# Layer 0's softmax sums from added key blocks, and one values evacuation moved ahead of a gate

## The chip, the cores and the metric

The kernel runs on one core of a Trainium2 chip. The metric is the device time of one execution in microseconds (us). A core has several engines that each run their own instruction stream in order and wait for each other through semaphores: TensorE (PE, matrix products, with its weight loads shown as PEld), VectorE (DVE), ScalarE (ACT), GpSimd (POOL) and SyncE (SP, which issues the DMAs here). SBUF is the working memory, PSUM the memory that matrix products are written to.

## What is computed

The input x has 128 rows of 256 positions and 256 channels. Two layers each add an attention of a group-normalized x to x. Layer 0, which the change touches, is attention along the 256 positions of each row, with 8 heads of 32 channels, a bias computed from a second tensor z, and a sigmoid gate:

```python
m_norm = layer_norm(m, ln_m_w, ln_m_b)          # m = group norm of x
q = (m_norm @ Wq.T).reshape(B, s, i, h, c)      # k and v likewise
b = (z_norm @ Wb.T).transpose(0, 3, 1, 2)[:, None]
gate = jax.nn.sigmoid(m @ Wg.T + bg)
scores = jnp.einsum('bsihc,bsjhc->bshij', q, k) * scale + b
p = jax.nn.softmax(scores, axis=-1)
o = jnp.einsum('bshij,bsjhc->bsihc', p, v).reshape(B, s, i, h * c)
o = o * gate
return o @ Wo.T + bo
```

Layer 1 is a banded attention (each position sees 16 neighbours on either side) and is not changed. Everything is float32.

## The kernel before

**Phases.** A first phase (to about 300 us) computes the bias, keeps its exponential in the tile `eb`, and takes the statistics of x. Layer 0 follows, to about 2436 us, then layer 1. At the end a few sums are checked (a second, general kernel would run if a check failed; it does not run here).

**Layer 0's pairs.** Rows are handled two at a time, in 64 pairs; a `Pair` object (line 1148) holds a pair's tiles. Positions are cut into two blocks of 128 keys (index b). A pair has four blocks of work (r, c): row r of the pair, and head group c with four heads. For each:

- `scores` (line 1242): eight matmuls with 32-row weights, four of them side by side in the array, give the scores transposed, with keys on partitions and queries along the free dimension, into two PSUM tiles of two heads each. ScalarE's Exp (line 1258) turns each into a tile e of 128x1024 (two heads, two key blocks, 256 queries).
- `add_bias` (line 1262): e is multiplied by `eb`, because the exponential of a sum is a product. The first two heads' tile goes to VectorE, the second to GpSimd (line 1266).
- `apply` (line 1268): matmuls with 32 columns of weights give, for each head, the values product (e with v) and the ones-product (e with a block of ones), which is the softmax's sum repeated over the head's 32 partitions. Both accumulate over the two key blocks, so there are eight matmuls of each kind. Each shows as two records in the profile.
- `invert` (line 1282): VectorE's reciprocal of the sums.
- `gate` (line 1287): VectorE computes gr = (gate + 1) times the reciprocal (line 1292) and multiplies it with the values product (line 1295).

Around these, `out_row` and `keep_row` project a finished row and add the residual (line 1317, from the PSUM tile ps_y), and a later pair is prepared: `centre`, `scale` and `residual` on GpSimd, `moments` and `norm` on VectorE, a small power on GpSimd (`root`), transposes (`turn`), projections (`project`) and values (`values`, `keep_values`, line 1236, from the PSUM tile ps_v).

**The order of the work** is written out by hand (the loop from line 1388): the call order is each engine's instruction order, and one pair's loop body has four stages, each starting with the `scores` of one block. `apply`, `invert` and `gate` of a block stand one stage after its `scores`; GpSimd's `scale` stands before its multiplication in the second stage, `centre` before that in the first, `residual` after it in the third. `some(n)` adds n waiting statistics instructions on VectorE; every four pairs queue 17 of them.

**Buffers.** The PSUM tiles for transposes, projections, values and output rows share two buffers (`mm`), so the n-th such tile waits until the n-2nd has been read. The e tiles have two buffers for each of the two tags; the tiles of `turn` have two.

Of the kernel before, what the change touches and what calls it, by code (L numbers as in the profile page):

```python
# [9 lines left out]
F32 = mybir.dt.float32  # L10
AF = mybir.ActivationFunctionType
ALU = mybir.AluOpType
# [4 lines left out]
P = 128  # L17
# [756 lines left out]
def fast_kernel(  # L774
# [25 lines left out]
    nc = tc.nc  # L800
    S, I, C = x.shape
    CZ = z.shape[2]
    H = wbT.shape[1]
    D0 = C // H
# [3 lines left out]
    NB = I // P  # L808
    KC = C // P
    NP = S // 2  # L810
    N2 = 2 * I
# [9 lines left out]
    ones = const.tile([P, P], F32, name="ones")  # L821
# [155 lines left out]
    with tc.tile_pool(name="pre", bufs=2) as pre, tc.tile_pool(  # L977
        name="pre1", bufs=1
# [5 lines left out]
        for w, dst in ((wq, qb), (wk, kb)):  # L984
            for m in range(KC):
                ps = pps.tile([P, 512], F32, name="b_ps", tag="mm")
                for k in range(KC):
                    nc.tensor.matmul(
                        ps[:, 0:1], w[:, k, m * P : (m + 1) * P], lnb_c[:, k : k + 1],
                        start=(k == 0), stop=(k == KC - 1),  # L990
# [142 lines left out]
    HQ = P // D0  # L1133
# [5 lines left out]
    with tc.tile_pool(name="l0", bufs=2) as sb, tc.tile_pool(  # L1139
        name="l0s", bufs=4  # L1140
    ) as sm, tc.tile_pool(name="ps_mm", bufs=2, space=PSUM) as ps_mm, tc.tile_pool(
        name="ps_s", bufs=2, space=PSUM
    ) as ps_s, tc.tile_pool(name="ps_o", bufs=2, space=PSUM) as ps_o:

        def mm(name):
            return ps_mm.tile([P, 512], F32, name=name, tag="mm")

        class Pair:
# [39 lines left out]


            def turn(self, src, name):  # L1190
                dst = sb.tile([P, KC, N2], F32, name=name, tag=name)
                for k in range(KC):
                    ps = mm("ps_x")
                    for t in range(NT):
                        nc.tensor.transpose(ps[:, t * P : (t + 1) * P], src[:, t, k * P : (k + 1) * P], ident)
                    nc.scalar.copy(dst[:, k, :], ps)  # L1196
                return dst
# [62 lines left out]
                return self.es  # L1260

            def add_bias(self, r, c, es):
                for a in range(2):
                    h = c * HQ + 2 * a
                    eng = nc.vector if a == 0 else nc.gpsimd
                    eng.tensor_tensor(es[a], es[a], eb[:, h : h + 2], ALU.mult)  # L1266

            def apply(self, r, c, es):

                o = ps_o.tile([P, 2, I], F32, name="ps_ov", tag="o")  # L1270
                for what in range(2):
                    for b in range(NB):
                        for q in range(HQ):
                            h = c * HQ + q
                            w = self.v[:, r, b, h * D0 : (h + 1) * D0] if what == 0 else ones[:, :D0]
                            nc.tensor.matmul(  # L1276
                                o[q * D0 : (q + 1) * D0, what, :], w, es[q // 2][:, q % 2, b, :],
                                start=(b == 0), stop=(b == NB - 1),
                            )
                self.o = o  # L1280

            def invert(self, r, c):
# [69 lines left out]
        def some(n):  # L1352
            for _ in range(min(n, len(later))):
                later.pop(0)()
# [10 lines left out]
        def pair(p):  # L1365
            return Pair(p) if p < NP else Nobody()

        now, nxt, nn = pair(0), pair(1), pair(2)
# [17 lines left out]
        with tc.manual_schedule():  # L1386
            was, es = Nobody(), None
            for p in range(NP):
                nn3 = pair(p + 3)

                e = now.scores(0, 0)
                nn.centre()
                now.add_bias(0, 0, e)
                was.apply(1, 1, es)
                was.invert(1, 1)
                was.gate(1, 1)
                nxt.turn_g()
                nxt.project("gT", 0)
                nxt.project("gT", 1)
                some(2)  # L1400
                es = e

                e = now.scores(0, 1)
                nn.scale()
                now.add_bias(0, 1, e)
                now.apply(0, 0, es)
                now.invert(0, 0)
                was.out_row(1)
                was.keep_row(1)
                now.gate(0, 0)  # L1410
                nxt.turn_n()
                nxt.project("qT", 0)
                some(1)
                es = e

                e = now.scores(1, 0)
                now.add_bias(1, 0, e)
                nn.residual()
                now.apply(0, 1, es)
                now.invert(0, 1)  # L1420
                now.gate(0, 1)
                nxt.values(0)
                nxt.keep_values(0)
                nn.moments()
                nn.root()
                nxt.project("kT", 0)
                nxt.values(1)
                nxt.keep_values(1)
                es = e

                e = now.scores(1, 1)
                now.add_bias(1, 1, e)
                now.apply(1, 0, es)
                now.invert(1, 0)
                now.out_row(0)
                now.keep_row(0)
                now.gate(1, 0)
                nn.norm(0)
                nn.norm(1)
                nxt.project("kT", 1)  # L1440
                nxt.project("qT", 1)
                some(2)
                es = e
                was, now, nxt, nn = now, nxt, nn, nn3
            was.apply(1, 1, es)
            was.invert(1, 1)
            was.gate(1, 1)
            was.out_row(1)
            was.keep_row(1)
            some(len(later))  # L1450
# [17 lines left out]
    with tc.tile_pool(name="l1", bufs=2) as sb, tc.tile_pool(  # L1468
        name="l1s", bufs=4
    ) as sm, tc.tile_pool(name="ps1_mm", bufs=2, space=PSUM) as ps_mm, tc.tile_pool(  # L1470
        name="ps1_s", bufs=2, space=PSUM
# [63 lines left out]
        def scores1(d, r):  # L1535

            es = []
            for c in range(KC):
                ps = ps_s.tile([P, 2, 512], F32, name="ps_sc1", tag="s")
                for b in range(NB):  # L1540
                    for q in range(2):
                        rs = slice(q * D1, (q + 1) * D1)
                        nc.tensor.matmul(  # L1543
                            ps[:, q, b * W : (b + 1) * W],
                            d["kT"][rs, c, r * I + b * P : r * I + (b + 1) * P],
                            d["qT"][rs, c, r * I + q0(b) : r * I + q0(b) + W],
                            start=True, stop=True,
                        )
                e = sm.tile([P, 2, NB * W], F32, name="e1", tag=f"e{c}", bufs=3)
                nc.scalar.activation(e, ps[:, :, : NB * W], AF.Exp)  # L1550
                nc.gpsimd.tensor_tensor(e, e, bcast(bw.rearrange("p b w -> p (b w)"), 1, 2), ALU.mult)  # L1551
                es.append(e)
            return es
# [56 lines left out]
        for p in range(NP):  # L1610
# [3 lines left out]
            for r in range(2):  # L1614
                es = scores1(d, r)
# [34 lines left out]
@with_exitstack  # L1650
def mixer_kernel(ctx, tc, *args):

    nc = tc.nc
    keep = ctx.enter_context(tc.tile_pool(name="verdict", bufs=1))
    verdict = keep.tile([1, 1], mybir.dt.int32, name="verdict")
    fast_kernel(tc, *args, verdict)
    again = nc.values_load(verdict[0:1, 0:1], min_val=0, max_val=1)
    with tc.If(again > 0):
        general_kernel(tc, *args)
# [53 lines left out]
```

## Time and profile before

| what | value |
|---|---|
| median of 3 runs | 3873.88 us (3872.06 to 3875.07) |
| the profiled execution's own time | 3873.13 us |
| its span, first to last instruction | 3871.4 us |
| TensorE busy | 3610.3 us, 93% of the span |
| VectorE busy | 2232.6 us, 58% |
| GpSimd busy | 1794.0 us, 46% |
| ScalarE busy | 1390.9 us, 36% |
| granted TensorE clock, mean | 0.976 |
| one pair of layer 0 (1004.52 to 1037.88 us) | TensorE 32.29 us busy of 33.36; VectorE 24.20; GpSimd 18.45; ScalarE 14.13 |

The profile is of one execution. A row of its timeline has the start, the busy time, the engine, the source line, the operation, out<-in by the program's tile names, shapes and count; in brackets stand the idle time before it and what ended that. In the groups of the page the columns are busy time in total, mean in nanoseconds, and idle time before with its releaser. An instruction that stands still for something other than a semaphore shows as busy: its duration grows, and no wait is shown.

### The profile page before, as it was taken

Reading aid. Unit: us, or ns where it says so; the run is one execution under the profiler, and the core shown is the slowest. Engines: PE = TensorE matmul, PEld = TensorE weight load, DVE = VectorE, ACT = ScalarE, POOL = GpSimd, SP = SyncE. Lnnn points to the kernel's source line nnn. Section 1 sums busy time; section 2 is a strip of 40 time slices with the busy share of each in tenths; the row PEclk is TensorE's granted clock in tenths of the full one; section 3 lists DMA queues with packets and bytes.
Section 4 is the critical chain, followed back from the end, with each engine's and each line's share of the span. In section 5 each row is a group of like instructions: output and inputs, shape, how many; then the busy total and the mean of one; then the engine's idle time right before and its main releaser. Section 6 shows DMA issues by size and latency. Waiting matters only on the chain. (4 is left out here: it accounts for less than half of the span.)

```text
span 3871.4 us, 67673 instructions
## 1 busy us (share of the span) xinstructions
PE 3610.3 (93%) x29510; PEld 2214.9 (57%) x29510; DVE 2232.6 (58%) x3461; ACT 1390.9 (36%) x1937; POOL 1794.0 (46%) x869
## 2 busy tenths in 40 slices
PE   5659999999999999999999999799999999999996
PEld 3325555555555555555555555466666666666664
DVE  5755777777777777777777777333333333333335
ACT  2324444444444444444444444222222222222221
POOL 2364555555555555555555554333333333333332
PEclk8779999999999999999999999899999999999998
DMA  9940101110110011011101100211111111111111
GB/s 288 320 142 10 36 18 40 39 40 18 40 40 31 25 35 39 18 39 40 40 18 39 40 22 14 66 45 56 45 56 45 56 45 56 45 56 45 56 40 47
DMA packets 189924, 211.82 MB, mean 55 GB/s; under 512 B 6320, under 2 KB 172208, under 8 KB 189488
## 3 DMA queue, kind: packets, MB, share of 16 engines
q1 hardware_dynamic: 189616, 207.38, 17.1%
q8 instruction: 233, 3.82, 0.4%
q14 instruction: 75, 0.61, 0.1%
HBM read 138.68 MB, written 68.68 MB: 54 GB/s over the span
## 5 line engine op out<-in xcount | busy, mean ns | idle before, releaser
L1266 POOL TENSOR_TENSOR e<-e,eb 128x1024 f32<-128x1024 f32 x256 | 633.8, 2476 | 925.4 <-ACT e L1258 925.4
L1266 DVE TENSOR_TENSOR e<-e,eb 128x1024 f32<-128x1024 f32 x256 | 317.1, 1239 | 563.8 <-ACT e L1258 563.8
L1258 ACT ACTIVATE e<-ps_sc 128x1024 f32<-128x1024 f32 x512 | 496.8, 1022 | 259.0 <-PE ps_sc L1249 255.5
L1551 POOL TENSOR_TENSOR e<-e,bw 128x576 f32<-128x576 f32 x256 | 355.3, 1410 | 468.1 <-ACT e L1550 468.1
L1508 PE MATMUL ps_p<-xgT,w_in 128*128 128x512 f32 x1024 | 502.1, 614 | 0.1
L1571 DVE RECIPROCAL rv<-ps_su 128x256 f32<-128x256 f32 x128 | 225.0, 1757 | 398.5 <-PE ps_su L1566 398.5
L1285 DVE RECIPROCAL rv<-ps_ov 128x256 f32<-128x256 f32 x256 | 448.0, 1750 | 0.0
L1493 POOL TENSOR_TENSOR xb<-xt,bout_r 128x1024 f32<-128x1024 f32 x64 | 151.4, 2367 | 406.1 <-DVE yo L1584 401.6
L1526 DVE TENSOR_TENSOR v<-ps_v,bv_r 128x512 f32<-128x512 f32 x128 | 88.5, 692 | 395.1 <-PE ps_v L1522 386.5
L1550 ACT ACTIVATE e<-ps_sc 128x576 f32<-128x576 f32 x256 | 152.8, 649 | 450.7 <-PE ps_sc L1543 449.9
L1249 PE MATMUL ps_sc<-qT,kT 32*128 32x256 f32 x4096 | 293.7, 400 | 0.0
L1249 PEld LDWEIGHTS ps_sc<-qT,kT 32*128 32x128 f32 x4096 | 185.3, 184 | 171.3 <-issue 165.7
L1230 PE MATMUL ps_v<-wv,xnT 128*128 128x256 f32 x1024 | 254.9, 392 | 26.1 <-DVE v L1236 26.1
L1276 PE MATMUL ps_ov<-e,v 128*32 128x256 f32 x4096 | 274.7, 385 | 3.2 <-DVE e L1266 2.4
L1508 PEld LDWEIGHTS ps_p<-xgT,w_in 128*128 128x128 f32 x1024 | 179.7, 190 | 166.9 <-issue 124.2
L1276 PE MATMUL ps_ov<-e,ones 128*32 128x256 f32 x4096 | 268.3, 379 | 0.0
L1310 PE MATMUL ps_y<-wo,oT 128*128 128x256 f32 x1024 | 257.1, 394 | 3.9 <-DVE oT L1295 3.9
L1215 PE MATMUL ps_p<-xgT,wg 128*128 128x512 f32 x512 | 238.2, 608 | 20.1 <-ACT xgT L1196 19.7
L1230 PEld LDWEIGHTS ps_v<-wv,xnT 128*128 128x128 f32 x1024 | 184.1, 189 | 124.6 <-DVE v L1236 78.3
L1219 ACT ACTIVATE kT<-ps_p,kb 128x512 f32<-128x512 f32 x128 | 88.0, 688 | 451.8 <-PE ps_p L1215 451.8
L1522 PE MATMUL ps_v<-w_in,xgT 128*128 128x256 f32 x1024 | 248.3, 385 | 0.0
L1215 PE MATMUL ps_p<-xnT,wq 128*128 128x512 f32 x512 | 245.7, 603 | 0.2 <-ACT xnT L1196 0.2
(145 smaller groups left out, 5558.5 us busy)
## 6 DMA issues: line engine op xcount, KB each, us to landing
xa<-in_x_dram SPq DMA_DIRECT2D x8, 4096.0 KB
xt<-in_x_dram SPq DMA_DIRECT2D x64, 512.0 KB
x<-xo SPq DMA_DIRECT2D x16, 2048.0 KB
xt<-x SPq DMA_DIRECT2D x64, 512.0 KB
out_dram<-yo SPq DMA_DIRECT2D x64, 512.0 KB
rsum<-rv SPq DMA_DIRECT2D x64, 16.0 KB
rsum<-rv SPq DMA_DIRECT2D x64, 8.0 KB
rs_all<-rsum SPq DMA_DIRECT2D x1, 1024.0 KB
```

The costliest lines, as they stand in the source:

```text
L1215: nc.tensor.matmul(ps, w[:, k, m * P : (m + 1) * P], getattr(self, src)[:, k, :], start=(k == 0), stop=(k == KC - 1),)
L1230: nc.tensor.matmul(self.ps_v[:, b * C : (b + 1) * C], self.xnT[:, k, t * P : (t + 1) * P], wv[:, k, :], start=(k == 0), stop=(k == KC - 1),)
L1249: nc.tensor.matmul(self.pss[q // 2][:, q % 2, b, :], self.kT[rs, c, r * I + b * P : r * I + (b + 1) * P], self.qT[rs, c, r * I : (r + 1) * I],
L1258: nc.scalar.activation(e, self.pss[a], AF.Exp)
L1266: eng.tensor_tensor(es[a], es[a], eb[:, h : h + 2], ALU.mult)
L1276: nc.tensor.matmul(o[q * D0 : (q + 1) * D0, what, :], w, es[q // 2][:, q % 2, b, :], start=(b == 0), stop=(b == NB - 1),)
L1285: nc.vector.reciprocal(self.rv[:, r, c, :], self.o[:, 1, :])
L1310: nc.tensor.matmul(self.ps_y[:, b * C : (b + 1) * C], self.oT[:, k, b * P : (b + 1) * P], wo[:, k, :], start=(k == 0), stop=(k == KC - 1),)
L1508: nc.tensor.matmul(ps, w_in[:, k, n * C + m * P : n * C + (m + 1) * P], xgT[:, k, :], start=(k == 0), stop=(k == KC - 1),)
L1522: nc.tensor.matmul(ps[:, b * C : (b + 1) * C], xgT[:, k, t * P : (t + 1) * P], w_in[:, k, 2 * C : 3 * C], start=(k == 0), stop=(k == KC - 1),)
L1551: nc.gpsimd.tensor_tensor(e, e, bcast(bw.rearrange("p b w -> p (b w)"), 1, 2), ALU.mult)
L1571: nc.vector.reciprocal(rv[:, r, :], su)
```

## The change

Three things change in layer 0. After each multiplication with `eb`, the same engine adds the two key blocks of the tile to a new tile `eboth` of 128x512 (one for each tag, two buffers). The ones-products run on that tile: four for each block of work instead of eight, with no accumulation. In the third stage the first values product is computed and evacuated before the gate of (0, 1) instead of after it; on TensorE this moves nothing, on VectorE the evacuation (line 1236) stands directly behind the reciprocal. The tiles of `turn` get one buffer instead of two.

```diff
-                dst = sb.tile([P, KC, N2], F32, name=name, tag=name)
+                dst = sb.tile([P, KC, N2], F32, name=name, tag=name, bufs=1)
...
                 for a in range(2):
                     h = c * HQ + 2 * a
                     eng = nc.vector if a == 0 else nc.gpsimd
                     eng.tensor_tensor(es[a], es[a], eb[:, h : h + 2], ALU.mult)
+                    both = sm.tile([P, 2, I], F32, name="eboth", tag=f"both{a}", bufs=2)
+                    eng.tensor_tensor(both, es[a][:, :, 0, :], es[a][:, :, 1, :], ALU.add)
+                    es.append(both)
...
-                for what in range(2):
-                    for b in range(NB):
-                        for q in range(HQ):
-                            h = c * HQ + q
-                            w = self.v[:, r, b, h * D0 : (h + 1) * D0] if what == 0 else ones[:, :D0]
-                            nc.tensor.matmul(
-                                o[q * D0 : (q + 1) * D0, what, :], w, es[q // 2][:, q % 2, b, :],
-                                start=(b == 0), stop=(b == NB - 1),
-                            )
+                for b in range(NB):
+                    for q in range(HQ):
+                        h = c * HQ + q
+                        nc.tensor.matmul(
+                            o[q * D0 : (q + 1) * D0, 0, :], self.v[:, r, b, h * D0 : (h + 1) * D0],
+                            es[q // 2][:, q % 2, b, :], start=(b == 0), stop=(b == NB - 1),
+                        )
+                for q in range(HQ):
+                    nc.tensor.matmul(
+                        o[q * D0 : (q + 1) * D0, 1, :], ones[:, :D0], es[2 + q // 2][:, q % 2, :],
+                        start=True, stop=True,
+                    )
...
                 now.invert(0, 1)
-                now.gate(0, 1)
                 nxt.values(0)
                 nxt.keep_values(0)
+                now.gate(0, 1)
                 nn.moments()
```

In the changed kernel the multiplication is line 1267, the addition line 1269, the values and ones-products lines 1278 and 1283, the reciprocal line 1292, the gate lines 1299 and 1302.

## The prediction

> **What bounds the kernel now.** I read the page's engine shares first (TensorE 93% busy), then the costliest groups, then the timeline of layer 0. All times are in us.
>
> ```profile
> L1266 POOL TENSOR_TENSOR e<-e,eb 128x1024 f32<-128x1024 f32 x256 | 633.8, 2476 | 925.4 <-ACT e L1258 925.4
> L1266 DVE TENSOR_TENSOR e<-e,eb 128x1024 f32<-128x1024 f32 x256 | 317.1, 1239 | 563.8 <-ACT e L1258 563.8
> L1285 DVE RECIPROCAL rv<-ps_ov 128x256 f32<-128x256 f32 x256 | 448.0, 1750 | 0.0
> L1276 PE MATMUL ps_ov<-e,ones 128*32 128x256 f32 x4096 | 268.3, 379 | 0.0
> ```
>
> The ones-products, which the change halves, hold TensorE for 268.3 in all. VectorE and GpSimd have long waits before their multiplications, so they look free. The timeline of one second stage (one of the four between two scores groups) shows whether they are:
>
> ```profile
> 1012.48 1.15 PE L1249 MATMUL ps_sc<-qT,kT 32*128 32x256 f32 x16
> ...
> 1014.71 1.23 DVE L1266 TENSOR_TENSOR e<-e,eb 128x1024 f32<-128x1024 f32 x1 [3.11 <-ACT e L1258]
> ...
> 1015.67 2.48 POOL L1266 TENSOR_TENSOR e<-e,eb 128x1024 f32<-128x1024 f32 x1 [2.98 <-ACT e L1258]
> 1015.86 1.75 DVE L1285 RECIPROCAL rv<-ps_ov 128x256 f32<-128x256 f32 x1
> ...
> 1017.52 0.63 DVE L1317 TENSOR_TENSOR xo<-ps_y,xt 128x512 f32<-128x512 f32 x1
> ...
> 1018.21 0.66 PE L1195 MATMUL ps_x<-ident,xn 128*128 128x128 f32 x4 [0.36 <-DVE xo L1317]
> ...
> 1020.59 0.50 PE L1249 MATMUL ps_sc<-qT,kT 32*128 32x256 f32 x4
> ```
>
> TensorE is full, but a VectorE chain runs close under it: exp, multiplication, reciprocal, evacuation of ps_y, and only then do the second transposes get their PSUM buffer (0.36 of wait already). I call the stages A (0,0), B (0,1), C (1,0), D (1,1). They take 7.96, 8.11, 8.99 and 8.30: 33.36 a pair, the same in every full pair. Offsets below count from a stage's first scores matmul. VectorE's multiplication starts at 2.24 and ends at 3.47, GpSimd's is asked for at 3.20 and ends at 5.68, and the reciprocal starts at 3.38.
>
> The view that decides is the end of layer 0, by engine:
>
> ```profile
> 2412.64 2.57 DVE L1266 TENSOR_TENSOR e<-e,eb 128x1024 f32<-128x1024 f32 x1
> ...
> 2418.47 3.29 DVE L1266 TENSOR_TENSOR e<-e,eb 128x1024 f32<-128x1024 f32 x1
> ```
> ```profile
> 2411.77 2.36 POOL L1266 TENSOR_TENSOR e<-e,eb 128x1024 f32<-128x1024 f32 x1 [0.47 <-ACT e L1258]
> 2418.33 2.34 POOL L1266 TENSOR_TENSOR e<-e,eb 128x1024 f32<-128x1024 f32 x1 [4.20 <-ACT e L1258]
> ```
>
> In these two blocks GpSimd's multiplication began ahead of VectorE's; no other VectorE multiplication of the 256 is longer than 1.3. VectorE's took 2.57 and 3.29 instead of 1.23, and ended 1.08 after GpSimd's end both times: it stood still until 0.14 before that end. In the other direction GpSimd's 2.48 against 2.35 undisturbed puts its start 0.14 before VectorE's end. The gate's first instruction (L1292) takes 0.79 instead of 0.41 where it meets that multiplication.
>
> [...]
>
> ```profile
> 2427.43:2430.84 3.41, 1.47 (x18) 0.50 (x10) 3.27 (x10) 0.00 (x0) 0.00 (x0) 1.00 0.01 2
> 2430.84:2434.25 3.41, 1.85 (x4) 1.50 (x5) 1.44 (x3) 0.00 (x0) 0.00 (x0) 0.50 0.02 5
> ```
>
> The columns are length, busy TensorE, weight loads, VectorE, ScalarE, GpSimd, granted clock. After a window with 1.47 busy the clock is 0.50.
>
> **The change part by part.**
>
> *Ones-products halved.* Values and ones products take 0.88 and 0.98 before the next matmul starts, 16 records each; 8 records fewer are 0.44. Over 256 blocks that is 113, all of it gained if nothing else binds.
>
> *VectorE's new addition,* 128x512, two SBUF inputs. Duration: oT's 256 elements take 0.424, the multiplication's 1024 take 1.225, so 512 take 0.69. It waits for its own multiplication (3.47), so it cannot ask before about 3.51. GpSimd asked for its multiplication at 3.20[...]. The addition is then blocked until 5.54 and ends at 6.23. Queued behind it in order is the reciprocal: 6.14 instead of 3.38, **2.76 later in every stage**. Bounds: 0.73 later if ports don't block it (0.69 plus 0.04), 2.76 if they do; I take 2.76, since the same engine, operation and operand kinds show it.
>
> *GpSimd's new addition.* Its 1024 elements take 2.37 (xb), 576 take 1.41, so 512 take 1.27. It runs at 6.09 to 7.36; the products that need it start in the next stage at about 1.96, so that wait is covered by two or more. But it pushes scale and residual to 7.32 to 9.67, and the gate's first instruction, asking at 7.92, is blocked until 9.53.
>
> *Stage A.* TensorE doesn't wait for VectorE here, and ScalarE is free for the xgT copies at 3.12, before the transposes end: 7.96 - 0.44 = 7.5. VectorE runs late: gate 9.53 to 10.40, two statistics to 11.07, which is 3.57 into B.
>
> *Stage B.* GpSimd asks at 3.20, now ahead: it runs 3.20 to 5.55, VectorE's multiplication 5.41 to 6.64, GpSimd's addition 6.50 to 7.77, VectorE's 7.63 to 8.32, reciprocal 8.23 to 9.98, ps_y out at 10.52. Before, the stage ended 2.44 after that evacuation: 12.96. Seventeen statistics entries fill twenty places in four pairs, so about one A in four has none; then VectorE is first (2.90 to 4.13), GpSimd 3.99 to 6.34, addition to 6.89, ps_y out 9.09, end 11.53. Mean 12.6.
>
> *Stage C.* Reciprocal to 7.89; the first values product, now ahead of the gate, is out at 8.48 (7.01 before); the second values product starts at 8.54 and the stage ends 1.92 later: 10.46. The move itself is worth up to 0.6 a pair in the old timeline (0.79 and 0.42 of gate no longer precede it); in the new one the gate would hold it until about 11. It moves no DMA: only the gate of (1,1) issues one, and SP's and GpSimd's queues keep their order. The gate's late result is needed 2.5 into D.
>
> *Stage D.* VectorE reaches D at 2.4, because statistics and the second values evacuation end late[...]. Multiplication 2.75 to 3.97, GpSimd's 3.83 to 6.18, addition 6.04 to 6.73, reciprocal to 8.39, ps_y out at 8.93, the q projection after it, end 1.81 after 8.99: 10.8.
>
> Sum 7.5 + 12.6 + 10.46 + 10.8 = 41.36 against 33.36: 8.0 a pair.
>
> *Clock.* In B TensorE has nothing from about 5.0 to 10.5[...]: 2.6 a pair.[...]
>
> *Buffers.* xgT and xnT keep one buffer each. xnT's last reader, D's q projection, stands before the next pair's copies in TensorE's own order by a whole stage, and xgT's by three; cost nothing, and the transposes' copies would wait if that cover were gone.
>
> Some 62 full pairs: (8.0 + 2.6) x 62 = 657 on the profiled execution's 3873.13, which is 0.75 under the median of the runs, so no correction: **4530**. Layer 1 stays.
>
> **Rivals.**
> 1. *Ports as above, but the clock stays up or its loss is hidden*: 3873 + 496 = 4369. For it: C and D wait for VectorE, so slower matmuls there may cost nothing. Against: scores and the last q projection of B lie on the chain.
> 2. *The addition follows its multiplication onto the ports at once, so only the 0.73 counts*: A 7.5; B 8.11 + 0.73 = 8.84; C: reciprocal to 5.86, values out at 6.45, second product from 6.51, end 1.92 later, 8.43; D: ps_y out at 6.41, the q projection at 6.47 where it stood at 6.49 anyway, 8.30. Sum 33.1, so 0.27 a pair less: 3856, **faster** by 0.4%. B and C grow one for one with the reciprocal's delay, D too from about 0.75, so it decides near 0.8 of delay. Against it: GpSimd is already asking when VectorE's multiplication ends (1015.67 against 1015.94)[...].
> 3. *No blocking of the addition, but the gate behind GpSimd's longer queue is late and reaches into B*: the gate of A would end some 0.5 to 1 after VectorE's turn in B. Rival 2's sum plus that is 3890 to 3920.
> 4. *GpSimd's addition becomes what TensorE waits for*: it would have to end after 1.96 of the next stage, and by the sums above it ends at least two earlier. A delay of 3 in all four stages would be 12 a pair; I give it no chance of its own.
>
> **How the numbers follow.** Main case 0.6, rival 1 0.27, rival 2 0.05, rival 3 0.08. About 0.2% (8 us) is what a measurement of this kernel tells from no change. The range holds main case and rival 1. Low end: rival 1's 4369 less 22, if B's fast order (12.96 - 11.53 = 1.43 shorter) comes in another quarter of the 62 pairs. High end: 4530 plus the clock's upper bound (0.8 x 62 = 50), plus B always in its slow order (0.36 x 62 = 22), plus 40 if the waits of 2 to 3 in C and D halve the clock too (0.65 a pair). That is 4350 to 4640. Faster 0.05 is rival 2; slower 0.93 is the rest but 0.02 for sums that cancel.
>
> **What would show it.** VectorE's additions (L1269) with a mean near 2.5 instead of 0.69; the reciprocal starting near 6.1 after the scores in A and C; waits of TensorE for xo in B and D and for v in C, each in the hundreds of us; TensorE busy well under 90% in layer 0, granted clock near 0.9 there; stage B longest. I would be wrong if L1269 on VectorE took 0.7, or if GpSimd's multiplication were the one that is delayed.

## The result and the profile after

The changed kernel takes 4455.52 us in the median (4454.62 to 4456.39, 4 runs), against 3874.48 us (3872.06 to 3875.1, 4 runs) for the kernel before: a ratio of 1.1501, with a 95% interval of 1.1481 to 1.1521. It is 15% slower, 581 us. The forecast was 4530 with a range of 4350 to 4640.

The costliest groups on the page of the changed kernel, with the columns of the page before (busy in total, mean in ns | idle before and its releaser):

```profile
L1269 DVE TENSOR_TENSOR eboth<-e 128x512 f32<-128x512 f32 x256 | 645.8, 2523 | 8.8
L1215 PE MATMUL ps_p<-xnT,wq 128*128 128x512 f32 x512 | 339.6, 799 | 376.0 <-DVE xo L1324 375.7
L1267 DVE TENSOR_TENSOR e<-e,eb 128x1024 f32<-128x1024 f32 x256 | 396.9, 1550 | 354.7 <-ACT e L1258 354.3
L1269 POOL TENSOR_TENSOR eboth<-e 128x512 f32<-128x512 f32 x256 | 429.9, 1679 | 20.1
L1230 PE MATMUL ps_v<-wv,xnT 128*128 128x256 f32 x1024 | 263.8, 402 | 143.5 <-DVE v L1236 143.5
L1299 DVE SCALAR_TENSOR_TENSOR gr<-gT,rv 128x256 f32<-128x256 f32 x256 | 349.8, 1366 | 2.3
```

VectorE's new addition takes 2523 ns in the mean. Its shortest is 691 ns: that is the work, and the rest is standing still. Before it there are only 8.8 us of idle time, because a blocked instruction counts as busy. TensorE now waits 375.7 us for the evacuation of ps_y (line 1324) and 143.5 us for that of ps_v (line 1236), where the same two evacuations cost it 22.2 and 26.1 us before. The chain of work that ended last, from the same page, runs largely over VectorE, on layer 0's lines (1269, 1292, 1267 and 1299 among them). The chain on the page before hardly reaches back into layer 0, so it gives no share to set beside this:

```profile
PE 45%; DVE 41%; issue 5%; ACT 4%; DMA 2%; POOL 2%; SPq 1%; ACTq 0%; POOLq 0%; DVEq 0%
```

A pair takes 42.6 us instead of 33.36. One second stage (B) in the timeline of the changed kernel; it is preceded by the end of A:

```profile
1027.76 2.36 POOL L1162 TENSOR_TENSOR xg<-xg,R_l 128x1024 f32<-128x1024 f32 x1
1027.98 1.15 PE L1249 MATMUL ps_sc<-qT,kT 32*128 32x256 f32 x16
...
1028.37 2.03 DVE L1299 SCALAR_TENSOR_TENSOR gr<-gT,rv 128x256 f32<-128x256 f32 x1
...
1031.17 2.35 POOL L1267 TENSOR_TENSOR e<-e,eb 128x1024 f32<-128x1024 f32 x1 [1.06 <-ACT e L1258]
1031.44 3.16 DVE L1267 TENSOR_TENSOR e<-e,eb 128x1024 f32<-128x1024 f32 x1
...
1033.60 2.12 POOL L1269 TENSOR_TENSOR eboth<-e 128x512 f32<-128x512 f32 x1
1033.65 0.66 PE L1195 MATMUL ps_x<-ident,xn 128*128 128x128 f32 x4 [0.73 <-ACT xnT L1196]
...
1034.64 1.63 DVE L1269 TENSOR_TENSOR eboth<-e 128x512 f32<-128x512 f32 x1
1036.19 1.75 DVE L1292 RECIPROCAL rv<-ps_ov 128x256 f32<-128x256 f32 x1
1037.86 0.62 DVE L1324 TENSOR_TENSOR xo<-ps_y,xt 128x512 f32<-128x512 f32 x1
...
1038.54 3.43 PE L1215 MATMUL ps_p<-xnT,wq 128*128 128x512 f32 x4 [4.24 <-DVE xo L1324]
...
1041.90 1.15 PE L1249 MATMUL ps_sc<-qT,kT 32*128 32x256 f32 x16
```

The gate of A (1028.37) stands still until GpSimd's scaling is done, so VectorE comes to B's multiplication 0.27 after GpSimd. VectorE's then takes 3.16 instead of 1.23, the two additions follow, GpSimd's (1033.60) ahead of VectorE's (1034.64), and TensorE has nothing for 4.24 us. What it does next, four records of the q projection, takes 3.43 us, most of it at half clock (0.51 from 1038.10 to 1041.53); at full clock, from 1018.54 in D, four take 1.98. The columns of the windows view are length, busy TensorE, weight loads, VectorE, ScalarE, GpSimd, and then the granted clock, the DMA engines' share and GB/s:

```profile
1034.70:1038.10 3.40, 0.00 (x0) 0.00 (x0) 3.40 (x3) 0.22 (x1) 1.02 (x1) 1.00 0.00 0
1038.10:1041.53 3.43, 2.99 (x4) 1.18 (x4) 1.47 (x4) 0.00 (x0) 0.00 (x0) 0.51 0.43 128
1041.53:1044.94 3.41, 3.41 (x43) 1.89 (x43) 0.81 (x1) 2.55 (x3) 0.00 (x0) 1.00 0.09 30
```

### The profile page after: what moved, and what is told of

It is laid out like the page before. It is cut to its first block, busy times and chain, and to the rows that moved or that the text cites. A ratio compares the mean times of both kernels' runs of the same rounds, so it can differ in the third digit from the quotient of the medians.

```text
span 4452.8 us, 64344 instructions
## 1 busy us (share of the span) xinstructions
PE 3670.1 (82%) x27462; PEld 2194.9 (49%) x27462; DVE 3035.3 (68%) x3717; ACT 1390.6 (31%) x1937; POOL 2192.6 (49%) x1125
## 4 chain that ended last, share of the span: by engine, by line
PE 45%; DVE 41%; issue 5%; ACT 4%; DMA 2%; POOL 2%; SPq 1%; ACTq 0%; POOLq 0%; DVEq 0%
PE ps_p L1515 11%; DVE eboth L1269 11%; DVE rv L1292 9%; DVE e L1267 9%; PE ps_p L1215 8%; PE ps_v L1529 5%; PE ps_y L1587 5%; DVE gr L1299 4%; PE ps_sc L1249 4%; PE ps_o L1573 4%; PE ps_sc L1550 3%; ACT e L1258 3%; DMA zt<-in_z_dram 2%; DVE xo L1324 2%; PE ps_su L1573 1%
## 5 line engine op out<-in xcount | busy, mean ns | idle before, releaser
L1269 DVE TENSOR_TENSOR eboth<-e 128x512 f32<-128x512 f32 x256 | 645.8, 2523 | 8.8
L1215 PE MATMUL ps_p<-xnT,wq 128*128 128x512 f32 x512 | 339.6, 799 | 376.0 <-DVE xo L1324 375.7
L1267 DVE TENSOR_TENSOR e<-e,eb 128x1024 f32<-128x1024 f32 x256 | 396.9, 1550 | 354.7 <-ACT e L1258 354.3
L1269 POOL TENSOR_TENSOR eboth<-e 128x512 f32<-128x512 f32 x256 | 429.9, 1679 | 20.1
L1230 PE MATMUL ps_v<-wv,xnT 128*128 128x256 f32 x1024 | 263.8, 402 | 143.5 <-DVE v L1236 143.5
L1215 PEld LDWEIGHTS ps_p<-xnT,wq 128*128 128x128 f32 x512 | 107.9, 233 | 529.8 <-DVE xo L1324 442.6
L1299 DVE SCALAR_TENSOR_TENSOR gr<-gT,rv 128x256 f32<-128x256 f32 x256 | 349.8, 1366 | 2.3
L1249 PE MATMUL ps_sc<-qT,kT 32*128 32x256 f32 x4096 | 336.3, 447 | 0.0
L1249 PEld LDWEIGHTS ps_sc<-qT,kT 32*128 32x128 f32 x4096 | 209.4, 209 | 223.9 <-issue 210.4
L1219 ACT ACTIVATE qT<-ps_p,qb 128x512 f32<-128x512 f32 x128 | 88.0, 687 | 633.8 <-PE ps_p L1215 633.8
```

The lines of the kernel that those rows point to most:

```text
L1215: nc.tensor.matmul(ps, w[:, k, m * P : (m + 1) * P], getattr(self, src)[:, k, :], start=(k == 0), stop=(k == KC - 1),)
L1230: nc.tensor.matmul(self.ps_v[:, b * C : (b + 1) * C], self.xnT[:, k, t * P : (t + 1) * P], wv[:, k, :], start=(k == 0), stop=(k == KC - 1),)
L1249: nc.tensor.matmul(self.pss[q // 2][:, q % 2, b, :], self.kT[rs, c, r * I + b * P : r * I + (b + 1) * P], self.qT[rs, c, r * I : (r + 1) * I],
L1269: eng.tensor_tensor(both, es[a][:, :, 0, :], es[a][:, :, 1, :], ALU.add)
L1299: nc.vector.scalar_tensor_tensor(gr, self.gT[:, c, r * I : (r + 1) * I], 1.0, self.rv[:, r, c, :], ALU.add, ALU.mult)
```

## The experiments

The theory under test: **VectorE's addition, with both operands in SBUF, stands still while GpSimd multiplies, as VectorE's multiplication did in two blocks of the kernel before (2.57 and 3.29 us instead of 1.23), and delays the reciprocal behind it; the halved clock adds to that.** In the prediction and the expectations this is the port theory. "Port" is the author's name; the traces show the standing still, and not what in the chip causes it. Rivals: the addition's own work in front of the reciprocal is enough, whatever it reads; the longer GpSimd queue is to blame; the moved evacuation, the halved products or the single buffers cost something; the clock's loss lies off the chain. All times are medians of 4 or 5 runs. The mean stage lengths come from the start of each group of scores products in the traces, without the first and last pairs:

| kernel | time | ratio to before (95%) | A | B | C | D | pair |
|---|---|---|---|---|---|---|---|
| before | 3874.5 | 1 | 7.96 | 8.12 | 8.99 | 8.30 | 33.36 |
| changed | 4455.5 | 1.1481 to 1.1521 | 7.53 | 13.44 | 10.98 | 10.64 | 42.59 |
| move alone | 3831.3 | 0.9871 to 0.9904 | 7.96 | 8.11 | 8.31 | 8.30 | 32.68 |
| no additions | 3750.0 | 0.9664 to 0.9696 | 7.53 | 8.12 | 7.88 | 7.87 | 31.38 |
| PSUM operand | 3860.7 | 0.9948 to 0.9976 | 7.53 | 8.64 | 8.46 | 8.43 | 33.06 |
| TensorE kept busy | 4328.5 | 1.1153 to 1.1190 | 7.53 | 12.05 | 10.41 | 10.44 | 40.42 |
| GpSimd's addition only | 3828.2 | 0.9868 to 0.9901 | 7.94 | 8.12 | 8.29 | 8.28 | 32.64 |
| VectorE's addition only | 4334.3 | 1.1173 to 1.1211 | 7.96 | 11.67 | 10.62 | 10.40 | 40.64 |
| late addition, late centring | 3763.5 | 0.9701 to 0.9733 | 7.53 | 8.12 | 7.88 | 7.97 | 31.49 |
| late addition alone | 4106.4 | 1.0586 to 1.0621 | 7.53 | 13.80 | 7.88 | 7.97 | 37.17 |
| GpSimd made to wait | 4049.4 | 1.0436 to 1.0471 | 7.53 | 10.93 | 8.84 | 8.86 | 36.15 |

### The move alone

```diff
                 now.invert(0, 1)
-                now.gate(0, 1)
                 nxt.values(0)
                 nxt.keep_values(0)
+                now.gate(0, 1)
```

> The kernel before with one edit: the first values evacuation stands ahead of the gate of (0, 1). Port theory (the additions cause the loss, the move is a gain): stage C 8.4 instead of 8.99, other stages as before, 0.5 to 0.6 a pair, so 3836 to 3845. Rival (the move delays a gate that something waits for): C no shorter or D longer, 3874 or more.

It took 3831.34 us, 43 less than before, all of it in C (8.31), so the move is a gain and not part of the loss. It is a little more than the 30 to 38 expected.

### No additions

```diff
                     eng.tensor_tensor(es[a], es[a], eb[:, h : h + 2], ALU.mult)
-                    both = sm.tile([P, 2, I], F32, name="eboth", tag=f"both{a}", bufs=2)
-                    eng.tensor_tensor(both, es[a][:, :, 0, :], es[a][:, :, 1, :], ALU.add)
-                    es.append(both)
...
-                        o[q * D0 : (q + 1) * D0, 1, :], ones[:, :D0], es[2 + q // 2][:, q % 2, :],
+                        o[q * D0 : (q + 1) * D0, 1, :], ones[:, :D0], es[q // 2][:, q % 2, 0, :],
```

> The changed kernel without both additions: the ones-products run on the first key block alone, so the sums leave out the second block. Port theory: TensorE saves 0.44 in each stage and nothing stands in front of the reciprocal; about 31.3 a pair, 3745 (3730 to 3770). Rival (half the ones-products, the single buffers or the move are to blame for the loss): well above 3874, up to the changed kernel's 4455.

It took 3750.00 us, as the port theory had it. The halved ones-products, the move and the single buffers together save 125 us; with the additions the kernel takes 705 us more. A, C and D each lose 0.43 of ones-products (0.44 was expected), C the move's 0.68 besides; only B stays at 8.12, where a chain over VectorE was under TensorE's work in the kernel before (0.36 us of wait for xo).

### An addition with a PSUM operand

```diff
+                    other = self.pss[0] if a == 0 else es[a]
-                    eng.tensor_tensor(both, es[a][:, :, 0, :], es[a][:, :, 1, :], ALU.add)
+                    eng.tensor_tensor(both, es[a][:, :, 0, :], other[:, :, 1, :], ALU.add)
```

> The changed kernel, with VectorE's addition taking its second operand from the PSUM tile of the scores (the raw scores of the second block instead of their weights), so same size, same place in the queue, same wait, but one SBUF input. Port theory: L1269 on VectorE near 0.69 instead of 2.52, reciprocal about 4.1 after the scores, and 3830 to 3890 in all. Rival (the addition's work and its wait on the multiplication in front of the reciprocal, whatever it reads): unchanged, 4400 to 4460.

It took 3860.68 us, 595 less than the changed kernel, with the same number of instructions on every engine. From its groups by line:

```profile
L1270 DVE TENSOR_TENSOR eboth<-e,ps_sc 128x512 f32<-128x512 f32 x256 | 176.0, 688 | 27.4 <-DVE e L1267 0.9
```

The addition takes 688 ns instead of 2523, and the reciprocal starts 4.17 (D) to 4.72 (A) after the scores. So it is neither the size, the place in the queue nor the wait on the multiplication: what costs is that both operands are in SBUF while GpSimd works (2523 ns; 688 with one of them in PSUM).

### TensorE kept busy

```diff
-                    for t in range(NT):
-                        nc.tensor.transpose(ps[:, t * P : (t + 1) * P], src[:, t, k * P : (k + 1) * P], ident)
+                    for again in range(1 + (warm if k else 0)):     # warm=6 in turn_n
+                        for t in range(NT):
+                            nc.tensor.transpose(ps[:, t * P : (t + 1) * P], src[:, t, k * P : (k + 1) * P], ident)
...
                 ps = mm("ps_p")
-                for k in range(KC):
+                for again in range(2 if which == "kT" else 1):
+                    for k in range(KC):
```

> The changed kernel with filler for TensorE in its gaps: the second group of transposes in B is done seven times, the k projections in C and D twice, all into the buffer they own. Theory that the halved clock lies on the chain: clock near 1.0 in layer 0, B's slow order 12.4, pair 40.4 instead of 42.6, 4320 (4300 to 4345). Rival (clock lost off the chain): clock near 1.0 and 4430 to 4470. If the filler itself delays B's fast order, up to 15 more than either.

It took 4328.53 us: repeated products that nobody needs make the kernel 127 us faster. The span and mean clock of its profiled execution (0.944 in the changed kernel):

```profile
core 0: 4326.7 us, clock 0.978
```

The standing still was left as it was (VectorE's addition still 2520 ns), so of the 581 us the halved clock is 127, or 2.17 of the 9.23 a pair, and the rest, 454, is there at full clock.

### One addition at a time

```diff
+                    if a == 1:     # a == 0 in the other run
                         both = sm.tile([P, 2, I], F32, name="eboth", tag=f"both{a}", bufs=2)
                         eng.tensor_tensor(both, es[a][:, :, 0, :], es[a][:, :, 1, :], ALU.add)
                         es.append(both)
...
+                        if q // 2 == 1 and b:     # == 0 in the other run
+                            continue
+                        src = es[2][:, q % 2, :] if q // 2 == 1 else es[q // 2][:, q % 2, b, :]
```

> The changed kernel with GpSimd's addition only: heads 2 and 3 of a block have two ones-products on the added tile, heads 0 and 1 four on the two key blocks; all sums complete. Port theory: the harm is in VectorE's addition, asked for while GpSimd multiplies; GpSimd's own delays only gates. TensorE saves 0.22 a stage and the move its 0.6: about 32.3 a pair, 3800 to 3825. Rival (the longer GpSimd queue is what costs, through the late gates): 3900 or more.

> The changed kernel with VectorE's addition only: heads 0 and 1 on the added tile, heads 2 and 3 on both key blocks; all sums complete. Port theory: reciprocal at about 6.1 in every stage as in the changed kernel, but gates end 1.2 earlier, so VectorE is ahead of GpSimd in B: A 7.7, B 10.7, C 10.9, D 10.3, 39.6 a pair, 4230 to 4310. Rival (VectorE's addition alone is harmless): under 3900.

With GpSimd's addition only it took 3828.19 us, with VectorE's only 4334.26. The harm starts with VectorE's: its reciprocal then starts 6.14 after the scores in A, B and D. GpSimd's addition alone does none: the time is that of the move alone (3831.34, overlapping intervals). Beside VectorE's it is not free, since the changed kernel takes 121 us more than the run with VectorE's only: the gate's first instruction stands still longer (1.37 in the mean instead of 0.50), VectorE's multiplication in B then comes second to GpSimd's (2.56 instead of 1.23), and B takes 13.44 instead of 11.67. Both runs were expected to save 0.22 of TensorE's time in each stage, and did not; A stayed at 7.94 and 7.96. This is the line for the ones-products on key blocks in the run with GpSimd's addition, from its groups by line, and the one of the changed kernel, which has halved ones-products throughout:

```profile
L1288 PE MATMUL ps_ov<-e,ones 128*32 128x256 f32 x2048 | 265.2, 379 | 0.0
```

```profile
L1283 PE MATMUL ps_ov<-eboth,ones 128*32 128x256 f32 x2048 | 158.5, 379 | 1.0 <-POOL eboth L1269 1.0
```

A block's eight ones-products are two rounds of four, which stand side by side in the array: in the kernel before, four records of 379 ns each take 0.40 us together (from 1014.44). Both lines have 2048 records. In the run with GpSimd's addition, 1024 more, on the added tile, stand beside those of the first round, and 265.2 us is what both rounds take (268.3 in the kernel before, with all 4096 records): two products of the second round are left out, and the two that stay take as long as four. In the changed kernel the whole second round is left out, and 158.5 us remain. VectorE's run missed its upper bound by 24 us; the excess lies in A, for this reason (7.96 instead of 7.7), and in B (11.67 instead of 10.7), where the q projection often took long too (3.53 us for four records; in the changed kernel 3.43 at mostly half clock and 1.98 at full clock).

### GpSimd made to wait

```diff
+                    if a == 1:
+                        tick = sm.tile([P, 4], F32, name="tick", tag="tick")
+                        eng.tensor_tensor(tick, es[2][:, 0, :4], mhalf[:, :4], ALU.mult)
                     eng.tensor_tensor(es[a], es[a], eb[:, h : h + 2], ALU.mult)
```

> The changed kernel with a small GpSimd instruction ahead of its multiplication that reads VectorE's new tile[...]; all the work is kept, and one instruction is added to each stage. Port theory (who asks first holds): L1269 on VectorE near 0.69, the reciprocal about 4.1 after the scores, GpSimd's multiplication 1.2 or more later than before, and 3860 to 3960 in all; the rest of the loss is GpSimd's late queue. Rival (the two engines together have too much work, in whatever order): 4300 or more.

It took 4049.44 us: less than half of the loss is left, but more than expected. The timeline of this run, C first, then B:

```profile
1005.00 0.69 DVE L1272 TENSOR_TENSOR eboth<-e 128x512 f32<-128x512 f32 x1
1005.61 1.75 DVE L1295 RECIPROCAL rv<-ps_ov 128x256 f32<-128x256 f32 x1
1005.77 0.20 POOL L1269 TENSOR_TENSOR tick<-eboth,mhalf 128x4 f32<-128x4 f32 x1 [4.54 <-DVE eboth L1272]
...
1005.93 2.35 POOL L1270 TENSOR_TENSOR e<-e,eb 128x1024 f32<-128x1024 f32 x1
...
1028.48 2.35 POOL L1162 TENSOR_TENSOR xg<-xg,R_l 128x1024 f32<-128x1024 f32 x1
1028.50 3.41 DVE L1270 TENSOR_TENSOR e<-e,eb 128x1024 f32<-128x1024 f32 x1 [0.67 <-ACT e L1258]
```

The addition now takes 0.69: GpSimd is held back by a semaphore until it is done (4.54 of wait), so no GpSimd instruction runs beside it. The expectation missed B. There GpSimd's late scaling starts 0.02 ahead of VectorE's multiplication, which then takes 3.41 (3.08 in the mean of all B stages) instead of 1.23.

### The addition later

```diff
-                    both = sm.tile([P, 2, I], F32, name="eboth", tag=f"both{a}", bufs=2)
-                    eng.tensor_tensor(both, es[a][:, :, 0, :], es[a][:, :, 1, :], ALU.add)
-                    es.append(both)
+                es += [None, None]
+                self.add_keys(es, 1)     # GpSimd's addition, behind both multiplications
...
-                nn.centre()              # these two lines not in the second run
                 now.add_bias(0, 0, e)
+                nn.centre()
...
                 now.gate(0, 0)           # and so behind the gate of every stage
+                now.add_keys(e, 0)       # VectorE's addition
```

> The changed kernel with VectorE's addition behind the gate of its stage instead of in front of the reciprocal, and GpSimd's centring of a later pair behind its multiplication and addition in A instead of in front (it ran in D). Port theory: [...]the reciprocal is at 3.4 again, and nothing reaches into the next stage: 31.3 a pair, 3745 to 3775, close to the kernel without additions (3750). Rival (VectorE and GpSimd have no room for the additions at any place): 3850 or more.

> As the run with the late addition, but the centring stays where it was. Port theory: in D VectorE's addition and four normalizations now meet GpSimd's addition and centring, VectorE comes late into A and then B[...]: B some 12 to 14.5, 4050 to 4180. Rival (only the place in front of the reciprocal matters): as the other, 3745 to 3775.

With both edits it took 3763.52 us, ratio 0.9717 (0.9701 to 0.9733): **faster than both kernels**, 2.8% under the kernel before, with the same computation as the changed kernel. The timeline of one C:

```profile
1015.78 1.23 DVE L1267 TENSOR_TENSOR e<-e,eb 128x1024 f32<-128x1024 f32 x1 [1.25 <-ACT e L1258]
...
1016.74 2.47 POOL L1267 TENSOR_TENSOR e<-e,eb 128x1024 f32<-128x1024 f32 x1 [1.42 <-ACT e L1258]
1016.92 1.75 DVE L1297 RECIPROCAL rv<-ps_ov 128x256 f32<-128x256 f32 x1
...
1018.59 0.63 DVE L1236 TENSOR_TENSOR v<-ps_v,vb_r 128x512 f32<-128x512 f32 x1
1019.13 0.41 DVE L1304 SCALAR_TENSOR_TENSOR gr<-gT,rv 128x256 f32<-128x256 f32 x1
1019.29 1.39 POOL L1274 TENSOR_TENSOR eboth<-e 128x512 f32<-128x512 f32 x1
...
1019.92 1.30 DVE L1274 TENSOR_TENSOR eboth<-e 128x512 f32<-128x512 f32 x1
```

The reciprocal and the evacuation of ps_v, both with a PSUM operand, now run during GpSimd's multiplication and take no longer for it (1.75 and 0.63; the shortest of the changed kernel are 1.74 and 0.62). VectorE's addition still stands still behind GpSimd's (1.30 instead of 0.69), but nothing urgent is queued behind it. The additions cost 13.5 us over the kernel without them.

Without the moved centring it took 4106.42 us, in the expected range. In the expected manner only in part: VectorE does come late from D into A, since its normalizations meet GpSimd's centring (0.91 for one in the mean, 0.42 in the changed kernel), but TensorE's largest wait is another. The timeline of that run:

```profile
1034.13 1.07 PE L1283 MATMUL ps_ov<-e,v 128*32 128x256 f32 x16 [1.97 <-DVE e L1267]
1038.57 1.08 PE L1288 MATMUL ps_ov<-eboth,ones 128*32 128x256 f32 x8 [3.37 <-DVE eboth L1274]
```

VectorE's addition of A itself lands so late that B's ones-products wait for it, 60 times in the run and 222.5 us in all.

## Why the prediction was right, and where its sum was off

**The mechanism and its sign were right.** The steps by their own numbers, from the scores of the stage, beside what the changed kernel's timeline shows:

| step | predicted | measured |
|---|---|---|
| reciprocal in A | 6.14 | 6.14 |
| gate of A done with its first instruction | 9.94 | 9.95 |
| VectorE's multiplication in B ends | 6.64 | 6.62 |
| VectorE's addition in B ends | 8.32 | 8.29 |
| ps_y out in B | 10.52 | 10.50 |
| ps_v out in C | 8.48 | 8.43 |
| ps_y out in D | 8.93 | 8.46 |
| A | 7.5 | 7.53 |

What carried the forecast is that VectorE's multiplication stood still beside GpSimd's in two blocks of the kernel before (2.57 and 3.29 us instead of 1.23), taken over to the addition. The PSUM-operand run agrees with it: 688 ns with one operand in PSUM against 2523 with both in SBUF. Also borne out: about one A in four gives B its fast order (18 of 62 full pairs have a B under 12). The mean of VectorE's addition was put near 2.5 and is 2.52.

**The sum was 75 us too high**, 4530 for 4455.5, in three terms. Per pair it was 41.36 at full clock and 2.6 for the clock. The run with TensorE kept busy separates them: 40.42 and 2.17. The three sizes that were off:

- *B's end, 0.55 too long* (12.6 against 12.05 at full clock). The step said that the second transposes wait for ps_y's PSUM buffer and that the stage ends 2.44 after its evacuation. In the changed kernel the second transposes take the buffer of the first ones (1033.65, released by ScalarE) and the q projection takes that of ps_y (1038.54), so less work is left behind the wait: B ends 1.97 after the evacuation in the run with TensorE kept busy. The program's two `mm` buffers were handed out in another order than before, so the rule that a tile waits for the reader of the last but one no longer holds there; the working had not looked at this.
- *D, 0.36 too long* (10.8 against 10.44). The step let VectorE's multiplication start only at 2.75, as if it stood still for the root on GpSimd; this was the author's estimate. It doesn't stand still, and ps_y is out at 8.46 instead of 8.93:

```profile
1011.87 1.02 POOL L1178 TENSOR_TENSOR lrs<-lrs,mhalf 128x4 f32<-128x4 f32 x1 [2.62 <-DVE lrs L1175]
...
1012.30 1.22 DVE L1267 TENSOR_TENSOR e<-e,eb 128x1024 f32<-128x1024 f32 x1
```

- *The clock, 0.43 too much* (2.6 against 2.17). The 2.6 was the author's estimate: the views shown of the kernel before have the clock at 0.50 behind a window with 1.47 us busy, and not how long it stays there. In 60 pairs of the changed kernel's trace the clock is halved for 5.06 a pair, but TensorE has products in only 4.61 of it, and half of that is 2.3. Nearly all of it reached the time: B, C and D have 1.45, 0.60 and 0.25 of it and are longer than at full clock by 1.39, 0.57 and 0.20. The reason given for rival 1, that later waits may hide the loss, holds for about 0.1 a pair.

These 1.34 over 62 pairs are 83 us. Against them stand some 9 us that the changed kernel lost in the first and last pairs, which the sum left out.

Of the rivals, 1 (no clock loss, 4369) is close to what the kept-busy run shows in its place, 4328.53, but the clock did count for 127. Rival 2, faster at 3856 if the addition were not blocked, is nearly the PSUM-operand run with its 3860.68. Its break-even at 0.8 of delay was set too low, since that run delays the reciprocal by 0.8 (C and D) to 1.3 (A) and still gains 14 us. B did not grow one for one there, but by 0.52 for a delay of 0.95: in it too the q projection has the buffer of ps_y, and B ends 1.97 after the evacuation instead of 2.44. Rival 3 differs from rival 2 by gates that reach into B; B grew by 0.52 there and not by more. Rival 4 did not come: TensorE's wait for GpSimd's addition is 1.0 us in all.

## What to carry to other kernels

An instruction that looks short and is placed on an idle engine has to be checked against what the other engine is doing at that moment, here VectorE against GpSimd. VectorE's instructions with two SBUF operands stood still for the rest of GpSimd's large ones (2523 ns instead of 691 for the addition), and so did what was queued behind them (the reciprocal in A at 6.14 after the scores instead of 3.38). In the profile this is no wait (8.8 us of idle time before the 256 additions) but a longer duration, so compare the shortest and the mean of one group. Put such an instruction behind those that feed TensorE, and use the GpSimd time for VectorE instructions with a PSUM operand (the reciprocal took 1748 ns in the mean in the run with the late addition and centring, 1750 in the kernel before). Then look for what the moved instruction meets in its new place: here that turned 15% slower into 2.8% faster, but only with GpSimd's centring moved as well; without it the kernel was 6% slower.

## What was not expected of the hardware

- A GpSimd instruction on 128x4 elements of 1.02 us did not hold up a VectorE instruction with two SBUF operands that started 0.43 after it (1.22, undisturbed 1.23; the same in all 47 pairs of the changed kernel in which they meet so), while those on 128x1024 did to within 0.14 of their end. So that small one did not hold VectorE up for the whole duration that the profile shows for it; whether it does for a part of it is not shown.
- Products with 32 columns of weights, four side by side in the array, took as long when two of the four were left out: with 12 of a block's 16 records of ones-products stage A took 7.94 (7.96 with all 16), and with 8, the second round left out as a whole, 7.53.
- Useless transposes and projections in TensorE's gaps gained 127 us, at a mean clock of 0.978 instead of 0.944. In the traces of the kernel before and of the changed one, the clock changes at distances that are multiples of 3.41 us. TensorE's busy time in stretches of that length between the changes: it was at most 47.0% in the 104 that a fall to half clock followed, and at least 41.8% in the 2115 at full clock that none followed; in between both occurred. So the stretch before a fall was not always idle: TensorE was busy for 1.47 of its 3.41 us once in the kernel before (from 2427.43), for 1.6 once in the changed one (from 355.40). The 102 stretches before a return to full clock were busy for at least 78.9%.
